# Self-attention and involution on one TensorE-bound core: v computed with pixels on partitions, and four smaller changes of order

## Chip, cores and metric

The kernel runs on one core of a Trainium2 chip. The metric is device time in microseconds, the median of three runs.

## What is computed

Two layers on x of shape (4, 512, 64, 64), all in f32. The first is single-head self-attention over the 4096 pixels of each image with 128 inner channels, and a residual. The second is an involution block: a 1x1 convolution to 128 channels with relu, then for every pixel a 7x7 filter for each of 8 groups of 16 channels, itself computed from that pixel, then a 1x1 convolution back to 512 channels and a residual.

```python
q = einsum('oc,bcn->bon', wq, xf) + bq            # k, v alike: 128 x 4096
attn = softmax(einsum('bci,bcj->bij', q, k), axis=-1)
out = einsum('bcj,bij->bci', v, attn)
x = einsum('oc,bcn->bon', wo, out) + bo + x
o = relu(affine(conv1x1(x, W1), s1, b1))          # 512 -> 128
w = conv1x1(relu(affine(conv1x1(o, Wr), sr, br)), Ws) + bs   # 49 taps x 8 groups
o = einsum('bgkhw,bgckhw->bgchw', w, patches(o))  # 7x7, zero padded
x = affine(conv1x1(o, W3), s3, b3) + x
```

## The kernel before, in words

All work is in `fast_path`; a second, general path runs only if a row sum of the softmax leaves a safe range, which it does not here. The images are done one after the other (L635). An image is eight chunks of 512 pixels.

**Keys and values** (`keys_values`, L420). For each chunk, four matmuls of 512 columns over the four channel tiles give pk (keys, channels on partitions), and four more give pv, values with channels on partitions. Attention needs v with pixels on partitions, so ScalarE copies pv to vs (L458), and one chunk later `turn` (L424) transposes it in four pieces on TensorE into pvt, which ScalarE copies to vT (L429). The bias of v is folded into the output bias: pb and bo, L639 to L643, once at image 0.

**Attention** (`attention`, L576). For each block of 512 queries (the last of the last image is cut into two of 256) there are 32 steps of 128 keys: a score matmul pss, exp on ScalarE into one of five pt buffers (L594), the product po with v, and on VectorE the sum of pt into pacc (L625); the last sum of a block is sums (L628).

**Finishing a block** (`finish_block`, L473) is a generator. Row sums become blocks, pl, rls and spread; four matmuls pwo (L511) are followed by four residual additions into x on VectorE (L513); then p1 (in the profile p, L520) and relu make the 128 channels, pp transposes them, and they are written to a padded image pix in DRAM (L548); pr and red prepare the filters. Each `yield` hands control back: one step is taken per call of `chores`.

**Involution** (`involution`, L280). A unit is four image rows with all 128 channels; an image has 16. The rows with their seven shifted copies are read from pix into a ring of 12 rows in SBUF (`pump`, L219: as many rows in one transfer as have been written and as the ring has room for). The filters of a unit are pw. For each tap column, VectorE multiplies 1, 2, 3 or 4 filter rows of ring data with pw into one of four prod buffers (L330), and GpSimd adds the product to acc (L354). After attention, in the tail, every second product is added on TensorE instead (accp, L350). `turn_unit` (L371) transposes acc (pa), and for every two units `close_chunk` (L401) does four matmuls py, four residual additions on VectorE (L408) and the store.

**The order of work** is written out by the Python program with a running estimate of TensorE's time, `pe`, in microseconds. `chores` (L248) is called after every step of attention and after every second matmul of keys and values; it takes one step of finishing, one of closing, and lets `pace` (L212) emit taps. `due` grows with TensorE's time; `involution` holds a tap back while VectorE's or GpSimd's estimated backlog is over 3.5 or 7.5 us, or its rows have not landed (L308). In the last image, `late` makes finishing wait for times instead of counting steps. Each engine takes its instructions in the order in which they were emitted, apart from small moves by the scheduler that builds the program. PSUM tiles pa, pwo, py, p, pp, pr, pl, spread and pq share two buffers, tag "mm"; acc and po have one each.

**The start.** vec goes on ScalarE's DMA queue; wk, then x of the first chunk in four pieces, wv, the next x and the other weights go on SyncE's (L171 to L179). GpSimd fills ones, the identity and zero.

Of the kernel before, what the change touches and what calls it, by code (L numbers as in the profile page):

```python
# [8 lines left out]
F32 = mybir.dt.float32  # L9
# [4 lines left out]
B, C, H, W = 4, 512, 64, 64  # L14
# [54 lines left out]
DVE_TAPS, POOL_TAPS = (0.16, 0.27), (0.19, 0.55)  # L69
ROW_US, X_US, PIX_US, LAND_US = 2.2, 3.8, 1.5, 3.0  # L70
HOP_US = 0.8
TB = 32

SAFE = (1e-30, 1e20)

# [2 lines left out]
def fast_path(  # L78
# [78 lines left out]
    def pe_us(us):  # L157
        nonlocal pe
        pe += us
# [8 lines left out]
        nc.sync.dma_start(xs[b, c], x_r[b, :, :, c * CH : (c + 1) * CH])  # L168


    nc.scalar.dma_start(vec, vecs)  # L171
    nc.sync.dma_start(wt[:, :O_WV], wts[:, :O_WV])
    c0, c1 = KEYS[:2]
    xs = {(0, c0): xpool.tile([P, CT, CH], F32, tag="x", name=f"x_0_{c0}")}
    for t in range(CT):
# [1 line left out]
    nc.sync.dma_start(wt[:, O_WV:O_WQ], wts[:, O_WV:O_WQ])  # L177
    load_x(0, c1)
    nc.sync.dma_start(wt[:, O_WQ:], wts[:, O_WQ:O_WR])  # L179
    nc.gpsimd.memset(ones, 1.0)  # L180
    make_identity(nc, ident)
    nc.gpsimd.memset(zero, 0.0)
    for i in range(P // TB):
# [8 lines left out]
    def w_slice(off, t):  # L192
        return wt[:, off + t * P : off + (t + 1) * P]
# [17 lines left out]

    def pace():  # L212
        nonlocal due, seen
        due, seen = min(due + TAPS_A_US * (pe - seen), 20), pe
        for _ in range(2):
            if due < 2 or not step(taps, 1):
                break

    def pump():  # L219

        nonlocal load
        while load // STEP in written:
            b, row = divmod(load, STEP)
            rows, us = written[b]

            end = H + SR - UR if rows == H else rows + PAD - 1
            n = min(b * STEP + end, low + RING) - load
            n = min(n, RING - load % RING)
            if n <= 0:
                break  # L230
            for h in range(2):
                src = pix[b % 2][row + h : row + h + n, :W, :]
                windows = bass.AP(
                    tensor=src.tensor, offset=src.offset, ap=[[P, W], [WP * P, n], [1, K * P]]
                )
                nc.sync.dma_start(
                    ring[h * W : (h + 1) * W, load % RING : load % RING + n]
                    .rearrange("p r x c -> p r (x c)"),
                    windows,
                )  # L240
            free["dma"] = max(free["dma"], us)
            us = takes("dma", ROW_US * n) + LAND_US
            landing.update((load + i, us) for i in range(n))
            load += n
            if row + n == H + SR - UR:
                load = (b + 1) * STEP
# [33 lines left out]
    def involution():  # L280
        nonlocal low, due
        while True:
# [15 lines left out]
            for o, (x, dy, n) in enumerate(ops):  # L298
                if o and dy >= DYS[1][0] > ops[o - 1][1]:
                    low = base + UR  # L300
                    pump()
                    if tail and units:
                        early[units[0]] = weights(*units[0])
                rows = [(base + dy + t * 2) % RING for t in range(NT)]
                while base + dy + n + NT > load:
                    yield "wait"
                landed = max(landing[base + dy + i] for i in range(n + NT))
                while not tail and (  # L308
                    pe < max(begin, landed)
                    or free["dve"] > pe + 3.5  # L310
                    or free["pool"] > pe + 7.5
                ):
                    yield "wait"
                free["pool"] = max(free["pool"], takes("dve", DVE_TAPS[0] + DVE_TAPS[1] * n))
                takes("pool", POOL_TAPS[0] + POOL_TAPS[1] * n)
                due -= n
                d0 = dy - DYS[dy >= DYS[1][0]][0]
                first = x == 0 and dy < DYS[1][0]
                prod, p0 = acc, d0
                if not first:  # L320
                    prod, p0 = prods.tile(
                        [P, NT, 4, P], F32, tag="prod", name=f"prod_{b}_{u}_{o}"
                    ), 0
                col = (x * K + dy) * G
                lines = ring[:, rows[0] : rows[0] + n, x, :]
                image = bass.AP(
                    tensor=lines.tensor, offset=lines.offset,
                    ap=[lines.ap[0], [(rows[1] - rows[0]) * K * P, NT], [K * P, n], [1, P]],
                )
                nc.vector.tensor_tensor(  # L330
                    prod[:, :, p0 : p0 + n, :].rearrange("p t d (g c) -> p t d g c", g=G),
                    image.rearrange("p t d (g c) -> p t d g c", g=G),
                    pw[:, :, col : col + n * G].unsqueeze(3)
                    .broadcast_to([P, NT, n * G, GC])
                    .rearrange("p t (d g) c -> p t d g c", d=n),
                    ALU.mult,
                )
                if first:
                    pass
                elif tail and o % 2 and (accp is not None or n > 1):  # L340

                    begin_sum = accp is None
                    if begin_sum:
                        accp = ps1.tile(
                            [P, NT, 2, P], F32, tag=("po", "acc")[u % 2], name=f"accp_{b}_{u}"
                        )
                    for d in range(0, n, 2):
                        k = min(2, n - d)
                        mm(
                            accp[:, :, :k, :], ident, prod[:, :, d : d + k, :],  # L350
                            begin_sum and d == 0, o + 2 >= len(ops) and d + 2 >= n,
                        )
                else:
                    nc.gpsimd.tensor_tensor(  # L354
                        acc[:, :, d0 : d0 + n, :], acc[:, :, d0 : d0 + n, :], prod[:, :, :n, :],
                        ALU.add,
                    )
                yield
# [61 lines left out]
    def keys_values(b):  # L420
        kt = kvpool.tile([P, N], F32, tag="k", name=f"k_{b}")
        vT = kvpool.tile([P, N // P, P], F32, tag="v", name=f"v_{b}")

        def turn(c, vs):  # L424
            pvt = ps1.tile([P, 4, P], F32, tag="acc", name=f"pvt_{b}_{c}")
            for j in range(4):
                nc.tensor.transpose(pvt[:, j, :], vs[:, j * P : (j + 1) * P], ident)
            pe_us(0.5)
            nc.scalar.copy(vT[:, 4 * c : 4 * c + 4, :], pvt)  # L429

        last = None
        for i, c in enumerate(KEYS):
            for k in KEYS[i + 1 : i + 3]:
                if (b, k) not in xs:
                    load_x(b, k)
            if b < 2 and i == 4:
                for rows in (slice(0, PAD), slice(PAD + H, None)):
                    nc.sync.dma_start(pix[b][rows].rearrange("r w c -> w r c"), zero)
                for cols in (slice(0, PAD), slice(PAD + W, None)):
                    nc.sync.dma_start(pix[b][PAD : PAD + H, cols, :], zero[:H])  # L440
            xt = xs[b, c] if c < KEEP else xs.pop((b, c))
            pk = ps_s.tile([P, CH], F32, tag="s", name=f"pk_{b}_{c}")
            for t in range(CT):
                mm(pk, w_slice(O_WK, t), xt[:, t, :], t == 0, t == CT - 1)
                if t % 2:
                    chores()
            nc.scalar.activation(
                kt[:, c * CH : (c + 1) * CH], pk, AF.Identity, bias=v1(V_BK)
            )
            if last is not None:  # L450
                turn(*last)
            pv = ps1.tile([P, CH], F32, tag="po", name=f"pv_{b}_{c}")
            for t in range(CT):
                mm(pv, w_slice(O_WV, t), xt[:, t, :], t == 0, t == CT - 1)
                if t % 2:
                    chores()
            vs = work2.tile([P, CH], F32, tag="q", name=f"vs_{b}_{c}")
            nc.scalar.copy(vs, pv)  # L458
            last = c, vs
        turn(*last)  # L460
        return kt, vT

    def queries(b, c, off, n):
# [9 lines left out]
    def finish_block(b, c, off, n, po, sums):  # L473
# [35 lines left out]
        for t in range(CT):  # L509
            pw = ps.tile([P, CH], F32, tag="mm", name=f"pwo_{name}_{t}")[:, :n]  # L510
            mm(pw, w_slice(O_WO, t), on)  # L511
            takes("dve", DVE_OP * n / CH)
            nc.vector.scalar_tensor_tensor(  # L513
                xt[:, t, :], pw, bo[:, t : t + 1], xt[:, t, :], ALU.add, ALU.add
            )
            for _ in range(t % 2 if late else 1 + (t != 1)):
                yield
        p1 = ps.tile([P, CH], F32, tag="mm", name=f"p1_{name}")[:, :n]
        for t in range(CT):
            mm(p1, w_slice(O_W1, t), xt[:, t, :], t == 0, t == CT - 1)  # L520
# [531 lines left out]
```

## Time and profile before

| | |
|---|---|
| time, median of 3 | 2656.51 us (2656.22 to 2658.48) |
| span of the profiled run | 2655.1 us |
| granted TensorE clock, mean | 0.997 |
| TensorE busy | 2625.3 us, 99% |
| VectorE, GpSimd, ScalarE busy | 1847.3, 1815.1, 886.5 us |
| DMA moved | 231.60 MB, mean 87 GB/s |
| ring reads, transfers of 1344 / 896 / 448 / 224 KB, median to landing | 15.3 / 13.4 / 8.7 / 3.3 us |

The profile is of one execution. Its parts are the busy time of each engine, the span in 40 slices, the DMA queues, the chain of work that ended last, the groups of instructions, and the DMA issues; the trace behind it answers for waits and for the timeline of any stretch. In those lines an instruction is named by line, tiles (out<-in) and shape; PE is TensorE's matmuls and PEld its weight loads, DVE VectorE, ACT ScalarE, POOL GpSimd. A line of the waits reads: engine, tile and line that waited <- what it waited for: microseconds in total, times, longest. A bracket at the end of a timeline line gives the engine's idle time before that group and what ended it. Each f32 matmul appears as two MATMUL and two LDWEIGHTS records.

### The profile page before, as it was taken

Reading aid. Unit: us, or ns where it says so; the run is one execution under the profiler, and the core shown is the slowest. Engines: PE = TensorE matmul, PEld = TensorE weight load, DVE = VectorE, ACT = ScalarE, POOL = GpSimd, SP = SyncE. Lnnn points to the kernel's source line nnn. Section 1 sums busy time; section 2 is a strip of 40 time slices with the busy share of each in tenths; the row PEclk is TensorE's granted clock in tenths of the full one; section 3 lists DMA queues with packets and bytes.
Section 4 is the critical chain, followed back from the end, with each engine's and each line's share of the span. In section 5 each row is a group of like instructions: output and inputs, shape, how many; then the busy total and the mean of one; then the engine's idle time right before and its main releaser. Section 6 shows DMA issues by size and latency. Waiting matters only on the chain.

```text
span 2655.1 us, 22780 instructions
## 1 busy us (share of the span) xinstructions
PE 2625.3 (99%) x6834; PEld 1197.4 (45%) x6834; DVE 1847.3 (70%) x2601; ACT 886.5 (33%) x1486; POOL 1815.1 (68%) x1195
## 2 busy tenths in 40 slices
PE   9999999999999999999999999999999999999998
PEld 4444444444444444444444444444444444444574
DVE  0347788786565777778566677778747577777877
ACT  2333333332333333333233333333323333333330
POOL 0007788787851878878774487878778277888865
PEclk9999999999999999999999999999999999999999
DMA  6032323235604233332450433333452423322243
GB/s 231 0 74 60 88 70 77 61 70 139 159 32 105 60 91 91 91 90 72 125 135 19 86 67 84 91 91 91 102 151 78 105 60 91 79 58 58 55 100 98
DMA packets 104260, 231.60 MB, mean 87 GB/s; under 512 B 5240, under 2 KB 23872, under 8 KB 104000
## 3 DMA queue, kind: packets, MB, share of 16 engines
q1 hardware_dynamic: 103984, 229.96, 35.2%
q8 instruction: 56, 0.92, 0.2%
q14 instruction: 76, 0.62, 0.1%
q10 hardware_dynamic: 144, 0.10, 0.0%
HBM read 187.28 MB, written 42.77 MB: 87 GB/s over the span
## 4 chain that ended last, share of the span: by engine, by line
PE 90%; POOL 4%; DMA 3%; DVE 2%; issue 1%; SPq 0%; ACT 0%; POOLq 0%; DVEq 0%; ACTq 0%
PE pss L200 33%; PE po L200 33%; PE p L200 4%; PE pwo L200 4%; PE py L200 4%; POOL acc L354 4%; PE pq L200 4%; DMA ring<-pix 2%; PE pw L200 2%; PE pv L200 2%; PE pk L200 2%; DVE prod L330 1%; DMA out_dram<-x 1%; PE accp L200 1%; PE pr L200 1%
## 5 line engine op out<-in xcount | busy, mean ns | idle before, releaser
L354 POOL TENSOR_TENSOR acc<-acc,prod 128x768 f32<-128x768 f32 (+3 forms) x1060 | 1693.2, 1615 | 814.6 <-DVE prod L330 629.5
L200 PE MATMUL pss<-q,k 128*128 128x512 f32 (+1 forms) x2112 | 1056.0, 585 | 0.0
L200 PE MATMUL po<-pt,v 128*128 128x512 f32 (+1 forms) x2112 | 1046.9, 580 | 0.0
L594 ACT ACTIVATE pt<-pss 128x512 f32<-128x512 f32 x1024 | 611.2, 597 | 1222.6 <-PE pss L200 1201.5
L625 DVE TENSOR_TENSOR pacc<-pacc,pt 128x512 f32<-128x512 f32 x958 | 666.1, 695 | 468.9 <-ACT pt L594 462.3
L330 DVE TENSOR_TENSOR prod<-ring,pw 128x512 f32<-128x512 f32 (+3 forms) x1092 | 898.8, 848 | 110.0 <-POOL acc L354 63.1
L200 PEld LDWEIGHTS po<-pt,v 128*128 128x128 f32 x2112 | 398.7, 190 | 478.5 <-issue 459.3
L200 PEld LDWEIGHTS pss<-q,k 128*128 128x128 f32 x2112 | 388.9, 190 | 454.6 <-issue 445.9
L408 DVE SCALAR_TENSOR_TENSOR x<-py,vec,x 128x512 f32<-128x512 f32 (+1 forms) x132 | 96.5, 732 | 64.5 <-PE py L200 62.3
L200 PE MATMUL py<-accT,wt 128*128 128x512 f32 (+1 forms) x264 | 131.7, 583 | 0.7 <-ACT accT L393 0.5
L200 PE MATMUL pwo<-on,wt 128*128 128x512 f32 (+1 forms) x264 | 129.9, 585 | 0.1
L200 PE MATMUL p<-x,wt 128*128 128x512 f32 (+1 forms) x264 | 122.5, 593 | 7.3 <-DVE x L513 7.3
L365 POOL TENSOR_TENSOR acc<-acc 128x512 f32<-128x512 f32 x120 | 119.8, 999 | 9.4
L200 PE MATMUL pk<-x,wt 128*128 128x512 f32 x256 | 119.5, 604 | 4.9 <-DMA x<-x_dram 4.9
L529 ACT ACTIVATE x<-x,vec 128x512 f32<-128x512 f32 (+1 forms) x132 | 92.9, 706 | 93.0 <-PE p L200 88.1
L200 PE MATMUL pv<-x,wt 128*128 128x512 f32 x256 | 116.8, 593 | 0.0
L200 PE MATMUL pq<-x,wt 128*128 128x512 f32 (+1 forms) x264 | 115.8, 579 | 0.0
L513 DVE SCALAR_TENSOR_TENSOR x<-pwo,bo,x 128x512 f32<-128x512 f32 (+1 forms) x132 | 95.9, 731 | 22.4 <-PE pwo L200 20.5
L330 DVE TENSOR_TENSOR acc<-ring,pw 128x1024 f32<-128x1024 f32 (+1 forms) x84 | 79.1, 961 | 46.5 <-PE pw L200 46.4
L200 PEld LDWEIGHTS p<-x,wt 128*128 128x128 f32 x264 | 50.6, 193 | 68.9 <-issue 56.8
L200 PEld LDWEIGHTS pwo<-on,wt 128*128 128x128 f32 x264 | 51.2, 194 | 61.5 <-issue 55.4
L200 PEld LDWEIGHTS pk<-x,wt 128*128 128x128 f32 x256 | 48.7, 194 | 64.6 <-issue 58.4
(58 smaller groups left out, 798.1 us busy)
## 6 DMA issues: line engine op xcount, KB each, us to landing
x<-x_dram SPq DMA_DIRECT2D x55, 1024.0 KB, 5.7
ring<-pix SPq DMA_DIRECT2D x32, 1344.0 KB, 15.3
ring<-pix SPq DMA_DIRECT2D x72, 448.0 KB, 8.7
out_dram<-x SPq DMA_DIRECT2D x31, 1024.0 KB, 4.2
ring<-pix SPq DMA_DIRECT2D x32, 896.0 KB, 13.4
ring<-pix SPq DMA_DIRECT2D x8, 2240.0 KB, 24.8
pix<-o1t SPq DMA_DIRECT2D x62, 128.0 KB, 2.5
ring<-pix SPq DMA_DIRECT2D x8, 224.0 KB, 3.3
```

The lines of the kernel that those rows point to most:

```text
L200: return nc.tensor.matmul(o, lhsT=lhsT, rhs=rhs, start=start, stop=stop)
L330: nc.vector.tensor_tensor(prod[:, :, p0 : p0 + n, :].rearrange("p t d (g c) -> p t d g c", g=G), image.rearrange("p t d (g c) -> p t d g c ...
L354: nc.gpsimd.tensor_tensor(acc[:, :, d0 : d0 + n, :], acc[:, :, d0 : d0 + n, :], prod[:, :, :n, :], ALU.add,)
L365: nc.gpsimd.tensor_tensor(acc[:, :, :n, :], acc[:, :, :n, :], acc[:, :, n : 2 * n, :], ALU.add)
L408: nc.vector.scalar_tensor_tensor(xt[:, t, :], py, v1(V_S3 + t), xt[:, t, :], ALU.mult, ALU.add)
L513: nc.vector.scalar_tensor_tensor(xt[:, t, :], pw, bo[:, t : t + 1], xt[:, t, :], ALU.add, ALU.add)
L529: nc.scalar.activation(xt[:, t, :], xt[:, t, :], AF.Identity, bias=v1(V_B3 + t))
L594: nc.scalar.activation(pt, pss, AF.Exp)
L625: nc.vector.tensor_tensor(paccs[k], paccs[k], pt, ALU.add)
```

## The change

1. **v at once.** The pixels of x become the stationary operand (128 of a chunk at a time) and wv the moving one, so that the product has pixels on partitions from the start: 16 matmuls of 128 columns instead of four of 512, in a PSUM tile that alternates between the tags po and acc; pvt and the copy to vs go.
2. **Pace.** `pace` may emit 2 taps plus one per microsecond of TensorE's time since the last call, instead of 2; in the last image VectorE's backlog may be 4.5 us instead of 3.5.
3. **Later use of the residual.** In all images but the last, two more steps go by between the last residual addition of a block and p1, which reads x.
4. **Lead-in.** Eight matmuls on ones, whose result nobody reads, are put ahead of everything on TensorE; ones is filled by VectorE; wk comes in two pieces on ScalarE's queue, ahead of vec, so that x is first on SyncE's.
5. **Ring rows by three.** In the last image one transfer into the ring holds at most three rows.

```diff
+STEP_US = 1.0
+PIECE = 3
+WARM = 8
...
+    for cols in (slice(0, P), slice(P, O_WV)):
+        nc.scalar.dma_start(wt[:, cols], wts[:, cols])
     nc.scalar.dma_start(vec, vecs)
-    nc.sync.dma_start(wt[:, :O_WV], wts[:, :O_WV])
...
-    nc.gpsimd.memset(ones, 1.0)
+    nc.vector.memset(ones, 1.0)
+
+    warm = ps.tile([P, P], F32, tag="mm", name="warm")
+    for _ in range(WARM):
+        nc.tensor.matmul(warm, lhsT=ones, rhs=ones, start=True, stop=True)
...
     def pace():
         nonlocal due, seen
+        steps = 2 + int((pe - seen) / STEP_US)
         due, seen = min(due + TAPS_A_US * (pe - seen), 20), pe
-        for _ in range(2):
+        for _ in range(steps):
...
-            n = min(n, RING - load % RING)
+            n = min(n, RING - load % RING, PIECE if b == B - 1 else RING)
...
-                    or free["dve"] > pe + 3.5
+                    or free["dve"] > pe + (4.5 if b == B - 1 else 3.5)
...
-        def turn(c, vs):
-            pvt = ps1.tile([P, 4, P], F32, tag="acc", name=f"pvt_{b}_{c}")
-            for j in range(4):
-                nc.tensor.transpose(pvt[:, j, :], vs[:, j * P : (j + 1) * P], ident)
-            pe_us(0.5)
-            nc.scalar.copy(vT[:, 4 * c : 4 * c + 4, :], pvt)
...
-            if last is not None:
-                turn(*last)
-            pv = ps1.tile([P, CH], F32, tag="po", name=f"pv_{b}_{c}")
-            for t in range(CT):
-                mm(pv, w_slice(O_WV, t), xt[:, t, :], t == 0, t == CT - 1)
-                if t % 2:
+            pv = ps1.tile([P, 4, P], F32, tag=("po", "acc")[i % 2], name=f"pv_{b}_{c}")
+            for j in range(4):
+                for t in range(CT):
+                    mm(
+                        pv[:, j, :], xt[:, t, j * P : (j + 1) * P], w_slice(O_WV, t),
+                        t == 0, t == CT - 1,
+                    )
+                if j % 2:
                     chores()
-            vs = work2.tile([P, CH], F32, tag="q", name=f"vs_{b}_{c}")
-            nc.scalar.copy(vs, pv)
-            last = c, vs
-        turn(*last)
+            nc.scalar.copy(vT[:, 4 * c : 4 * c + 4, :], pv)
...
+        for _ in range(0 if late else 2):
+            yield
         p1 = ps.tile([P, CH], F32, tag="mm", name=f"p1_{name}")[:, :n]
```

More of the change, by code (lines that the diff above doesn't have):

```diff
@@ L422, in keys_values @@
         vT = kvpool.tile([P, N // P, P], F32, tag="v", name=f"v_{b}")
-        def turn(c, vs):
-            pvt = ps1.tile([P, 4, P], F32, tag="acc", name=f"pvt_{b}_{c}")
-            for j in range(4):
-                nc.tensor.transpose(pvt[:, j, :], vs[:, j * P : (j + 1) * P], ident)
-            pe_us(0.5)
-            nc.scalar.copy(vT[:, 4 * c : 4 * c + 4, :], pvt)
-        last = None
         for i, c in enumerate(KEYS):
```

## The prediction

> **What bounds the kernel now.** I read the page's first part, then the waits of the TensorE, then the timeline of the start, of the first image change, and of the end.
>
> ```profile
> PE 2625.3 (99%) x6834; PEld 1197.4 (45%) x6834; DVE 1847.3 (70%) x2601; ACT 886.5 (33%) x1486; POOL 1815.1 (68%) x1195
> PE p L200 <- DVE x L513: 7.3, 3, 2.5
> PE pk L200 <- DMA x<-x_dram: 4.9, 1, 4.9
> PE accp L200 <- DVE prod L330: 4.0, 4, 2.3
> PE pw L200 <- DVE prod L330: 2.1, 2, 1.4
> ```
>
> TensorE is the bound until attention ends (last sums at 2564.11): up to there it waits only for its first operands (4.9 us), three times for p at image changes (7.3) and for a few pw. After it, the last four units' taps on VectorE run to 2639.27, and a chain of copies, py and stores ends at 2655.1. So three things count: TensorE's work, its waits, and how many taps are left for the tail.
>
> ```profile
> 2564.11 0.69 DVE L628 TENSOR_TENSOR sums<-pacc,pt 128x512 f32<-128x512 f32 x1 [1.03 <-ACT pt L594]
> 2639.27 1.06 DVE L271 TENSOR_SCALAR ok<-rls 128x512 f32<-128x512 f32 x1
> ```
>
> ```profile
> 4.88 6.20 PE L200 MATMUL pk<-x,wt 128*128 128x512 f32 x8 [4.88 <-DMA x<-x_dram]
> 17.79 0.60 PE L427 MATMUL pvt<-ident,vs 128*128 128x128 f32 x4
> 18.22 3.60 PE L200 MATMUL pv<-x,wt 128*128 128x512 f32 x8
> 66.77 0.97 PEld L200 LDWEIGHTS pb<-vec,wt 128*128 128x128 f32 x8
> 2642.49 1.05 PE L200 MATMUL pa<-ident,acc 128*128 128x128 f32 x8
> 2643.38 0.61 PE L200 MATMUL pa<-ident,accs 128*128 128x128 f32 x4
> 2643.82 1.06 PE L200 MATMUL pa<-ident,acc 128*128 128x128 f32 x8
> 2644.72 0.61 PE L200 MATMUL pa<-ident,accs 128*128 128x128 f32 x4
> ```
>
> Columns: start, time, engine, instruction. Each f32 matmul shows as two passes. Eight passes of 512 columns take 3.43 us start to start (0.429 each), the first pk 6.2; four transposes 0.43; 20 passes of 128 columns with a new weight each (2642.49 to 2644.72) 2.23, or 0.1115 each. Eight loads for pb, whose products have one column, take some 0.89: 0.111 each, so a weight load sets that rate.
>
> The first image change, time from E = 626.03, the end of the old image's last po:
>
> ```profile
> 624.10 13.15 POOL L354 TENSOR_TENSOR acc<-acc,prod 128x768 f32<-128x768 f32 x7 [3.94 <-DVE prod L330]
> 637.33 2.08 POOL L365 TENSOR_TENSOR acc<-acc 128x512 f32<-128x512 f32 x2
> 639.96 27.75 POOL L354 TENSOR_TENSOR acc<-acc,prod 128x1024 f32<-128x1024 f32 x13 [0.55 <-DVE prod L330]
> 658.30 0.95 DVE L330 TENSOR_TENSOR prod<-ring,pw 128x768 f32<-128x768 f32 x1 [0.93 <-POOL acc L354]
> 659.18 0.74 DVE L513 SCALAR_TENSOR_TENSOR x<-pwo,bo,x 128x512 f32<-128x512 f32 x1
> 659.97 1.98 PE L200 MATMUL p<-x,wt 128*128 128x512 f32 x4 [2.42 <-DVE x L513]
> ```
>
> GpSimd adds without a pause; each product needs one of four prod buffers; the fourth residual (x at L513) stands on VectorE behind such a product; p needs it, also because p's PSUM tile is the one pwo held.
>
> **The skill.** "TensorE: Matmul & The Clock Gate", LDWEIGHTS, prices a weight load by its columns, 128/1.2 = 107 ns, and lets it run under the matmul before it; the trace has 0.111 for f32. The same page, Part 1, says that the array starts at half rate and is released after about 3.4 us of activity: the first pk's passes are 0.85 apart, later ones 0.43, and the switch falls near 9.7, 4.8 us after the start. Its table of queues has VectorE as strict FIFO, which the residual behind the products shows.
>
> **The change, part by part.**
>
> *v at once.* Removed per chunk: 8 passes of 512 (3.43), 4 transposes (0.44), one ScalarE copy. Added: 32 passes of 128: 3.57 at 0.1115. Saved 0.30 a chunk, 32 chunks: 9.6 us. Bounds: 0.107 a pass, the transposes' pace, gives 14; 0.118, at which the 16 pa passes from 2606.63 to 2608.52 went, gives 3. ScalarE loses a copy of 0.58 a chunk and is 33% busy: nothing on the path. At image 0 also the wait for vs before pb (0.73) goes. So image 0: 8 x 0.30 + 0.7 = 3.1.
>
> *Lead-in.* Eight f32 matmuls on ones are 16 passes; at half rate 0.22 each, from about 1.0 to 4.5, while wk and x land. If release follows activity as before, it comes near 6 rather than 9.7: pk starts near 4.5, has under two cold passes, ends near 8.7 instead of 11.0. Saved 2.3 (1 to 3.3). wk as two pieces on the ScalarE queue starts x 0.46 sooner; within that. By the bytes moved, the second x is in by 10.7, and is needed at 12.3.
>
> *Image change (two more yields).* In the built order p moves behind the next pv, but the py of an older chunk (the second of four) now takes the PSUM tile that pwo's fourth held, and its wait in the built program is that fourth residual. When is it there? VectorE now has all seven 768-element products of unit 11 behind sums and blocks, whose end is near E-0.4. GpSimd then starts at E+0.5: 13.15 + 2.08 + six 1024 adds (2.43 each, 14.6) + one 768 (1.88), then a product 0.95 and the residual 0.7: E+33.9. When is it wanted? TensorE has 3.43+0.14+3.57+3.43+0.86 (pk, pl, pv, pk, pw), 3.57+0.86 (pv, pwo), 3.43+1.72 (pk, two pwo), 0.22+3.57 (pa, pv), 1.72 (pwo, py), 3.43 (pk): E+30.0. It waits 3.9, against 2.4 before. (Same sums for before: residual 659.9, p wanted 657.4: as seen.) Behind that py stand pv, p and all of the phase. The residual chain belongs to GpSimd, so what v saves before the wait is waited again. Whole phase, E to the first pss: 80.3 before; after, 2.4 less for v, 0.9 for a pw that moves later (not saved), 0.7 for its wait, 2.4 for p's wait, plus 3.9 and 0.8 for q's copy that nothing covers now: net -0.8 each, three: -2.4. The later pix write (E+51 instead of E+46) delays ring rows to about E+74; pacc's first copy then comes near E+84, and the five pt buffers need it by E+87: no wait.
>
> *Pace.* A step of attention is four passes, 1.72 us, so three taps instead of two may go per call; the guard of 3.5 us is unchanged for images 0 to 2, the taps done by the end of each block are the same within 20 rows, and VectorE (70%) and GpSimd (68%) work beside TensorE: nothing. For image 3 the guard is 4.5: VectorE may lag 1 us more. Behind the longer queue stand pacc, which frees pt for the next exp, and the residuals of pwo, which free the PSUM tiles of later pwo; TensorE waits for both. Before, no such wait shows in image 3; there are nine blocks, so taken +1, bounds 0 to 4.
>
> *Tail.* I counted the taps that stand behind the last blocks in VectorE's built order, in output rows of one filter row: 196 before (four whole units of 49), 165 after. The 31 are seven products of 1024 (1.13 apart) and one of 768 (0.87); one py residual (0.67) goes ahead too: 9.4 us less VectorE work behind the last sums. But the seven come in a burst ahead of it: from one pacc to sums stand five pacc (0.6 each), seven products (7.9) and the py residual (0.7), 11.6, where TensorE takes five steps of 1.72, 8.6; and the first waits some 0.5 for its pw. So the last sums run 3.5 late, and the tail ends 5.9 earlier (3 to 9: with the lag doubled, or with none). VectorE's pauses in the tail, some 6 us in all, I leave as they are. Rows by three cuts up loads: two-row loads take 8.7 (median), four-row ones 13.4, and the first row that unit 14's second half needs from a freed slot is wanted some 15 us after the slot is free; hidden, with little to spare, so no gain and no loss. The last 16 us, from the end of the taps to the end of the stores, are the same instructions.
>
> Sum: -3.1 - 2.3 - 2.4 + 1.0 - 5.9 = -12.7, from 2656.5: 2644.
>
> **Rivals.**
> (A) The wait at image changes is gone: taps' products start earlier, or the py is not held. Then 3 x 3.9 more: about 2632. For: p had only 2.4 to lose, and the two yields are meant for it. Against: the PSUM tile and the sums above. Chance 0.2.
> (B) What the burst and the guard win in taps is lost again in image 3 (pacc behind products, residuals late), and the tail gains nothing: +3 and 0 instead of +1 and -5.9: 2652. For: the waits of VectorE's products for GpSimd are 63 us already, and whatever stands behind such a product waits too. Against: five pt buffers bear five steps, 8.6 us, of lag. Chance 0.16.
> (C) Slower: weight loads do not hide under 128-column passes. At 0.19 + 0.107 a pass, pv costs 9.5 a chunk instead of 3.57, 32 chunks +190: about 2834. A milder form, 0.13 a pass because x as weights and a PSUM tile shared with attention disturb the flow, costs 1024 passes x 0.0185 = +19: 2663. Speaks for it that one load alone lasts 190 ns; against it the pa groups, whose passes with a new weight each start 0.1115 apart. Together 0.08.
> Mine 0.56.
>
> **How the numbers follow.** 2644 is the likeliest. The range 2630 to 2654 takes in A and B and the ends of v (-4.6 more), tail and lead-in; C is left out. Faster than 2651.2: mine, A and 0.05 of B, 0.81; between 2651.2 and 2661.8: the rest of B, 0.11; slower: C, 0.08.
>
> **What would show it.** v: 32 passes of pv in 3.5 to 3.6 us. Lead-in: first pv near 8.7. Image change: no wait of p, but three waits of py for x at L513's counterpart, about 4 us each; if py waits under 1 us, A is right. Image 3: TensorE waits over 1 us in all before the last sums speak for B. Tail: from the end of attention to the end 82 us, before 88. Wrong most likely where GpSimd's chain starts elsewhere than E+0.5, since every us of it moves the time by three.

## The result, and the profile after

The changed kernel takes 2644.95 us (median of 5, 2644.45 to 2645.81) against 2658.48 (5 runs, 2656.22 to 2661.26) for the kernel before on the same chip: ratio 0.9948, 95% interval 0.9937 to 0.996. The profiled spans are 2643.6 and 2655.1 us. By stages of the two timelines, in us:

| stage | before | after | difference | forecast |
|---|---|---|---|---|
| start to the first pss of image 0 | 72.21 | 67.09 | -5.12 | -5.4 |
| three image changes, first pk to first pss | 80.42, 81.60, 82.88 | 80.57, 81.89, 80.83 | -1.61 | -5.0 |
| attention of images 0 to 2, pss to next pk | 1679.86 | 1680.21 | +0.35 | +1.7 |
| image 3, first pss to last sums | 567.14 | 570.68 | +3.54 | +5.4 |
| last sums to the end of the taps (ok) | 75.16 | 67.18 | -7.98 | -9.4 |
| from there to the end | 15.83 | 15.15 | -0.68 | 0 |
| sum | | | -11.5 | -12.7 |

The prediction's -0.8 an image change counts a pw of 0.86 us back in, because it only moves behind the first scores. By stages its terms are thus -1.7 an image change and +0.86 in each attention that follows. The traces have the pw there: each image change has 8 passes of pw instead of 12, the attention of images 1 and 2 has 56 instead of 52, and image 3 from its first pss on 72 instead of 68.

The lines of after that answer to those shown of before. First the page's busy times, then TensorE's waits (total, times, longest):

```profile
PE 2614.5 (99%) x7478; PEld 1254.9 (47%) x7478; DVE 1851.5 (70%) x2602; ACT 870.0 (33%) x1454; POOL 1821.4 (69%) x1197
```

```profile
PE py L208 <- DVE x L513: 12.7, 3, 4.5
...
PE pss L208 <- ACT q L469: 2.3, 3, 0.8
```

The three waits of p (7.3) are gone; three waits of py for the same residual stand in their place, and they are longer. TensorE's timeline, at the start and at the first image change:

```profile
1.64 3.20 PE L188 MATMUL warm<-ones 128*128 128x128 f32 x14
4.63 4.74 PE L208 MATMUL pk<-x,wt 128*128 128x512 f32 x8
9.21 3.73 PE L208 MATMUL pv<-wt,x 128*128 128x128 f32 x32
...
646.97 3.60 PE L208 MATMUL pk<-x,wt 128*128 128x512 f32 x8
654.52 1.30 PE L208 MATMUL py<-accT,wt 128*128 128x512 f32 x2 [3.95 <-DVE x L513]
655.61 5.24 PE L208 MATMUL pv<-wt,x 128*128 128x128 f32 x32
660.69 1.88 PE L208 MATMUL p<-x,wt 128*128 128x512 f32 x4
```

The first pv starts at 9.21 and the next pk at 12.78: 3.57 for 32 passes. After the wait of py the same 32 passes take from 655.61 to 660.69, 5.08. VectorE and GpSimd at that change, and VectorE at the end:

```profile
652.85 0.95 DVE L339 TENSOR_TENSOR prod<-ring,pw 128x768 f32<-128x768 f32 x1 [0.93 <-POOL acc L363]
653.72 0.75 DVE L513 SCALAR_TENSOR_TENSOR x<-pwo,bo,x 128x512 f32<-128x512 f32 x1
...
2561.27 0.68 DVE L630 TENSOR_TENSOR sums<-pacc,pt 128x512 f32<-128x512 f32 x1
2628.45 1.06 DVE L280 TENSOR_SCALAR ok<-rls 128x512 f32<-128x512 f32 x1
```

```profile
621.11 13.17 POOL L363 TENSOR_TENSOR acc<-acc,prod 128x768 f32<-128x768 f32 x7 [4.96 <-DVE prod L339]
634.36 2.08 POOL L374 TENSOR_TENSOR acc<-acc 128x512 f32<-128x512 f32 x2
636.40 27.75 POOL L363 TENSOR_TENSOR acc<-acc,prod 128x1024 f32<-128x1024 f32 x13
```

GpSimd adds without a pause, the fourth residual stands behind a product that waits for GpSimd, and it ends 34.15 us after the last po. The slow passes after the wait show in the table of stretches, whose third number from the end is the granted clock:

```profile
core 0: us, PE busy (x) PEld busy (x) DVE busy (x) ACT busy (x) POOL busy (x), PEclk, DMA share, GB/s
654.40:657.90 3.50, 3.38 (x13) 2.77 (x14) 2.85 (x5) 0.00 (x0) 3.34 (x3) 0.64 0.00 0
1299.40:1302.90 3.50, 3.39 (x10) 2.36 (x11) 2.86 (x5) 0.00 (x0) 3.34 (x3) 0.50 0.00 0
```

In the kernel before, four passes of p take 1.82 us behind its first wait, but 3.51 and 3.09 behind the second and third, whose lines the prediction does not show. The second:

```profile
1303.52 3.68 PE L200 MATMUL p<-x,wt 128*128 128x512 f32 x4 [2.45 <-DVE x L513]
1307.03 1.03 PE L200 MATMUL py<-accT,wt 128*128 128x512 f32 x2
```

Two questions come out of this. Is the wait of py made by the PSUM tile that it takes, and does it bring the half-rate passes with it? And is each part worth what the sum gave it?

### The profile page after: what moved, and what is told of

Its sections match the earlier page's. It is cut to its first block, busy times and chain, and to the rows that moved or that the text cites. A ratio compares the mean times of both kernels' runs of the same rounds, so it can differ in the third digit from the quotient of the medians.

```text
span 2643.6 us, 24069 instructions
## 1 busy us (share of the span) xinstructions
PE 2614.5 (99%) x7478; PEld 1254.9 (47%) x7478; DVE 1851.5 (70%) x2602; ACT 870.0 (33%) x1454; POOL 1821.4 (69%) x1197
## 4 chain that ended last, share of the span: by engine, by line
PE 91%; POOL 4%; DMA 2%; DVE 2%; issue 1%; ACT 0%; SPq 0%; POOLq 0%; DVEq 0%; ACTq 0%
PE pss L208 32%; PE po L208 32%; POOL acc L363 4%; PE pq L208 4%; PE p L208 4%; PE py L208 4%; PE pwo L208 4%; PE pv L208 3%; PE pk L208 3%; DMA ring<-pix 2%; PE pw L208 2%; DVE prod L339 1%; PE pr L208 1%; PE pp L543 1%; PE accp L208 0%
## 5 line engine op out<-in xcount | busy, mean ns | idle before, releaser
L208 PE MATMUL py<-accT,wt 128*128 128x512 f32 (+1 forms) x264 | 133.0, 587 | 13.8 <-DVE x L513 12.7
L208 PEld LDWEIGHTS pv<-wt,x 128*128 128x128 f32 x1024 | 123.3, 198 | 14.8 <-issue 14.8
L208 PE MATMUL pv<-wt,x 128*128 128x128 f32 x1024 | 126.0, 282 | 0.0
L531 ACT ACTIVATE x<-x,vec 128x512 f32<-128x512 f32 (+1 forms) x132 | 92.9, 706 | 81.5 <-PE p L208 76.3
L208 PEld LDWEIGHTS py<-accT,wt 128*128 128x128 f32 x264 | 49.5, 191 | 72.9 <-issue 43.3
L208 PEld LDWEIGHTS pq<-x,wt 128*128 128x128 f32 x264 | 49.7, 190 | 58.8 <-issue 52.7
```

The costliest lines, as they stand in the source:

```text
L208: return nc.tensor.matmul(o, lhsT=lhsT, rhs=rhs, start=start, stop=stop)
L531: nc.scalar.activation(xt[:, t, :], xt[:, t, :], AF.Identity, bias=v1(V_B3 + t))
```

## The experiments

**1. What does the wait of py cost?** Closing (pa, py) is held at image changes from the fourth pwo until p is issued, so no second py takes that pwo's PSUM tile; and a variant with one more step before p.

```diff
+    def chores(kv=False):
         step(finishing, 1)
-        step(closing, 1)
+        if not (kv and held):
+            step(closing, 1)
...
+        if not late:
+            held.append(name)
         for _ in range(0 if late else 2):      # 3 in the variant
             yield
+        held.clear()
         p1 = ps.tile(...)
```

> The changed kernel, but at image changes closing (pa and py) stops from the fourth pwo until p is issued, so that the second py does not take the PSUM tile of the fourth pwo. Theory (the tile makes the wait of 3.95 to 4.55 us, and that wait costs another 1.5 to 2 us of half-rate passes): p is wanted about 3.6 us later than that py was, waits 0.3 to 1 us for the residual, no half-rate passes follow, and three times 4.7 to 5.5 us are saved: 2629 to 2631. Rival (what is saved is waited again before the next image's scores, for q, ring rows or pacc): 2640 or more.

> As the kernel with closing held from the fourth pwo until p, with three steps instead of two before p, so that half a pk goes ahead of p as well. Theory: p does not wait at all, 3 x 5 to 6 us saved against the changed kernel: 2627 to 2630, some 1 us less than with two steps. Rival: py heaps up later in the image change or the next image's rows come too late for pacc, and it is slower than with two steps.

Measured: 2628.05 us with two steps (ratio to before 0.9887, 0.9872 to 0.9902), 2624.1 with three (0.987, 0.9855 to 0.9885), both below what was expected. TensorE's timeline with two steps, the three places where p waits, and VectorE's residual there:

```profile
653.81 1.98 PE L209 MATMUL p<-x,wt 128*128 128x512 f32 x4 [0.31 <-DVE x L515]
...
1293.70 1.98 PE L209 MATMUL p<-x,wt 128*128 128x512 f32 x4 [1.00 <-DVE x L515]
...
1932.89 1.98 PE L209 MATMUL p<-x,wt 128*128 128x512 f32 x4 [0.64 <-DVE x L515]
```

```profile
652.14 0.95 DVE L341 TENSOR_TENSOR prod<-ring,pw 128x768 f32<-128x768 f32 x1 [0.94 <-POOL acc L365]
653.01 0.74 DVE L515 SCALAR_TENSOR_TENSOR x<-pwo,bo,x 128x512 f32<-128x512 f32 x1
```

The residual ends 34.1 us after the last po, as in the changed kernel; only its first user comes later. The wait falls from 12.7 to 2.0 us in all, the passes after it run at full rate (p's four take 1.82), and the three image changes last 75.3, 76.3 and 75.6 us instead of 80.6, 81.9 and 80.8. That is 16.1 us less, 10.7 of waiting and 5.4 of half-rate passes. py reads accT and wt and not x, so its tile alone ties it to the residual: the PSUM tile made the wait, and nothing took it back. With three steps p does not wait at all, but not for the reason I gave:

```profile
647.53 0.74 DVE L515 SCALAR_TENSOR_TENSOR x<-pwo,bo,x 128x512 f32<-128x512 f32 x1
...
654.45 1.88 PE L209 MATMUL p<-x,wt 128*128 128x512 f32 x4
```

There the built order also has three products fewer ahead of the residual, which ends at 648.27, over 6 us before p needs it.

**2. Is it the idle that slows the passes?** TensorE is kept active in the wait (the pv tile is made earlier for it, which the cut leaves out):

```diff
+                if b and i == 3 and t == 3:
+                    for _ in range(15):
+                        nc.tensor.matmul(pv[:, 0, :], lhsT=ones, rhs=ones, start=True, stop=True)
                 if t % 2:
                     chores()
```

> The changed kernel with 15 matmuls of 128 columns on ones (30 passes, 3.35 us; nobody reads them) into the next pv tile ahead of the py that waits at each image change. The residual that py waits for comes no sooner. Theory (an idle of some 4 us puts TensorE back to half rate for about 3.4 us): with TensorE active in the wait, the 32 passes of pv after it take 3.6 us instead of 5.1, the rest of the wait is 0.5 to 1.2 us, and the time is 4 to 5.7 us less: 2639 to 2641. Rival (the passes after the wait are slow for another reason, such as their operands or what VectorE does then): those 32 passes take 5 us as before, and the time does not move.

Measured: 2641.36 us, ratio 0.9935 (0.9921 to 0.9948), against 0.9948 for the changed kernel: some 3.5 us less, though the intervals overlap. The timeline at the first change, and the granted clock behind the py at all three:

```profile
654.58 1.12 PE L209 MATMUL py<-accT,wt 128*128 128x512 f32 x2 [0.97 <-DVE x L517]
655.54 3.73 PE L209 MATMUL pv<-wt,x 128*128 128x128 f32 x32
659.11 1.88 PE L209 MATMUL p<-x,wt 128*128 128x512 f32 x4
```

```profile
654.50:659.10 4.60, 4.52 (x34) 4.04 (x35) 3.16 (x5) 0.00 (x0) 4.37 (x4) 1.00 0.00 0
1298.70:1303.30 4.60, 4.53 (x34) 4.05 (x35) 3.15 (x5) 0.00 (x0) 4.37 (x4) 1.00 0.00 0
1943.40:1948.00 4.60, 4.52 (x34) 4.04 (x35) 3.16 (x5) 0.00 (x0) 4.37 (x4) 1.00 0.02 4
```

py starts at the same time as before, so the residual came no sooner; the 32 passes after it take 3.57 at a clock of 1.00. The rival cause falls. The gain is under the forecast: full rate saves 5.4 us at the three changes, but pa now waits 2.3 us at two of them.

**3. Each part taken out of the changed kernel.** In turn: the old v; no added steps; no matmuls on ones and the old DMA order; two taps per call and a guard of 3.5; ring rows as many as fit.

```diff
-        for _ in range(0 if late else 2):                 # no added steps
-            yield
...
-        steps = 2 + int((pe - seen) / STEP_US)            # old pace
+        steps = 2
...
-                    or free["dve"] > pe + (4.5 if b == B - 1 else 3.5)
+                    or free["dve"] > pe + 3.5
...
-            n = min(n, RING - load % RING, PIECE if b == B - 1 else RING)    # rows as fit
+            n = min(n, RING - load % RING)
```

> The changed kernel with the old making of v (four 512-column products, four transposes, two copies a chunk); all else as changed. My theory (the TensorE time per chunk is what counts, 3.43 + 0.44 against 3.57): 9.6 us more over 32 chunks, plus 0.7 for the wait before pb, less some 0.9 at each of three image changes, because what v saves ahead of the waiting py is waited again: 7 to 8 us slower than the changed kernel, 2652 to 2653; the wait of the second py for the fourth residual about 3.0 us each instead of 3.95 to 4.55. Rival (the new v buys nothing, because weights from x and PSUM tiles shared with attention cost elsewhere what it saves): within 2 us of the changed kernel.

> The changed kernel without the two added steps between the last residual and p, so that p is again what waits for the fourth residual. Theory 1 (the wait belongs to the residual, which GpSimd's chain of adds sets, and only moves from p to py): p waits 2.5 to 3.1 us at each image change, no py waits, and the time is 1 to 4 us less than the changed kernel, 2641 to 2644, because one more py lies ahead of the wait. Theory 2 (the two steps do what they are for): 3 x 2 us or more slower, 2651.

> The changed kernel without the eight matmuls on ones, with the old DMA order and GpSimd filling ones. Theory: pk starts near 4.9 and passes at half rate, first pv at 11.0 instead of 9.2: 1.9 us slower, all of it in the first 12 us, 2647. Rival: a later wait (x of the second chunk, or the weights) takes it back, and the time does not move.

> The changed kernel with two taps per call and a guard of 3.5 us in the last image too. Theory (31 row-taps more are left for the tail, last sums 3.5 us earlier): 4 to 6 us slower, 2649 to 2651, with the end of the taps about 9 us later after the last sums. Rival B (a burst ahead of the last sums costs there what the tail wins): within 1.5 us of the changed kernel.

> The changed kernel with ring rows of the last image again in transfers of as many rows as fit. Theory (transfers are hidden): within 1 us of the changed kernel. Rival (rows come too late for the taps in the tail, and three at a time start them sooner): 2 us or more slower, with waits of products for the ring in the last 120 us.

| without | time | ratio to before (95%) | image changes |
|---|---|---|---|
| v at once | 2656.03 | 0.9991 (0.9985 to 0.9998) | 82.42, 84.69, 84.26 |
| the two steps | 2646.95 | 0.9957 (0.9943 to 0.997) | 83.22, 82.73, 82.83 |
| the lead-in | 2647.64 | 0.9955 (0.9942 to 0.9969) | 81.14, 81.75, 81.27 |
| pace and guard | 2656.54 | 0.9993 (0.9986 to 1.0) | 85.68, 85.51, 85.65 |
| rows by three | 2647.12 | 0.9958 (0.9945 to 0.9972) | 81.92, 82.49, 81.31 |

The ratios less 0.9948 come to some 11, 2, 2, 12 and 3 us; the five add to 30, over twice the 13.8 that 0.9948 stands for. The intervals of the three small ones overlap that of the changed kernel; the two large ones stand clear of it and alone make 23. So the parts are not separate terms. With the old v, py waits 3.25, 4.25 and 3.94 us, not the 3.0 that I expected, and the slow passes after it cost 6.6 us in all, so that it is 11 us and not 7 to 8. Without the lead-in the first pv starts at 10.13 and the first pss at 68.02, against 66.4 to 67.1 in eight runs with lead-in and the new v: 0.9 to 1.6 us. In the changed kernel pk starts 0.24 us sooner than without the lead-in, and its eight passes take 4.58 instead of 5.26, so most of the gain is in the rate of the passes. Without rows by three image 3 and its tail are 0.4 us longer; another 2.4 us lie at the image changes, where TensorE's order is the same in both: behind waits of the same length (12.5 and 12.7) half-rate passes lose 7.8 us instead of 5.7. A difference of 2 to 3 us between two kernels can thus come from the half-rate passes alone. The surprise is the pace. TensorE's waits and one line of its timeline without it:

```profile
PE pk L208 <- DMA x<-x_dram: 22.1, 3, 7.5
```

```profile
692.75 5.28 PE L208 MATMUL pk<-x,wt 128*128 128x512 f32 x8 [7.53 <-DMA x<-x_dram]
```

No py waits for a residual any more; pk waits for x, and runs at half rate after it (5.1 us for 3.43). Neither of my theories had this wait. Without the two steps it is there too (11.8 us in all), and p waits 3.6 us in all, less than half of what I expected. The tail is as short as in the changed kernel (66.6 us), so the pace is not what shortened it.

**4. Where does the wait for x come from?** SyncE's queue at the first change without the pace (time, length, line, transfer):

```profile
666.31 1.26 SPq L550 DMA_DIRECT2D pix<-o1t  x2
668.97 0.39 SPq L426 DMA_DIRECT2D out_dram<-x  x1
669.46 3.46 SPq L245 DMA_DIRECT2D ring<-pix  x4
673.01 0.63 SPq L171 DMA_DIRECT2D x<-x_dram  x1
```

and in the changed kernel:

```profile
670.25 0.38 SPq L426 DMA_DIRECT2D out_dram<-x  x1
673.36 1.26 SPq L550 DMA_DIRECT2D pix<-o1t  x2
674.72 0.56 SPq L171 DMA_DIRECT2D x<-x_dram  x1
675.85 4.38 SPq L245 DMA_DIRECT2D ring<-pix  x6
```

In the changed kernel the image's last x (1 MB) goes out ahead of all ring rows and lands 8.1 us after its issue. Without the pace it goes out behind four ring transfers (2.7 MB) and lands 19.6 us after it. To test whether the place is the cause, the old pace is kept and only this load is emitted one chunk sooner, which leaves TensorE's order as it was but for one pw at each image change, which moves behind the first scores:

```diff
-            for k in KEYS[i + 1 : i + 3]:
+            for k in KEYS[i + 1 : i + (4 if i == 4 else 3)]:
```

> The changed kernel with the old pace and guard, as in the run without them, and one thing more: the load of an image's last chunk of x is emitted one chunk earlier, which moves it ahead of the four transfers of ring rows on SyncE's queue and leaves TensorE's order as it was. Theory Q (the wait of pk for x, 7.3 to 7.5 us three times, comes from that place in the queue): the wait is gone, and with it the half-rate passes after it: 22 to 28 us less than without the pace, 2628 to 2635. Rival (the x is late because its buffer comes free late, and the place does not matter): pk waits as before, within 3 us of 2656.5. Second rival (ring rows come later by as much, and pacc or the taps wait instead): 2645 or more.

Measured: 2631.58 us, ratio 0.9898 (0.9882 to 0.9913), 25 us less than with the load in its old place. The queue, the pk that had waited, and VectorE around the fourth residual:

```profile
665.96 1.26 SPq L550 DMA_DIRECT2D pix<-o1t  x2
668.62 0.39 SPq L426 DMA_DIRECT2D out_dram<-x  x1
670.67 0.37 SPq L171 DMA_DIRECT2D x<-x_dram  x1
671.10 7.43 SPq L245 DMA_DIRECT2D ring<-pix  x6
...
684.71 3.60 PE L208 MATMUL pk<-x,wt 128*128 128x512 f32 x8
```

```profile
649.09 0.95 DVE L339 TENSOR_TENSOR prod<-ring,pw 128x768 f32<-128x768 f32 x1 [1.47 <-POOL acc L363]
649.97 0.74 DVE L513 SCALAR_TENSOR_TENSOR x<-pwo,bo,x 128x512 f32<-128x512 f32 x1
```

The load goes out only 2.3 us earlier, and pk no longer waits for it. The last two lines show what the new pace does at an image change: with the old one the residual starts at 649.97, behind three 768-element products after the last 1024-element one; with the new one at 653.72, behind five. Two products at GpSimd's 1.88 us are 3.76; counted from the last po the residual is 3.4 us later. With the old pace the second py is also wanted 1.6 us later (31.9 us after the last po, not 30.2). Most of the wait of py in the changed kernel is thus made by its pace.

**5. v alone, rows by three alone**, each put on the kernel before.

> The kernel before with the new making of v and nothing else. In its built order the load of the last chunk of x of each image change stands on SyncE's queue behind the store of an old chunk and behind transfers of ring rows, where in the kernel before and in the changed kernel it stands ahead of all ring rows. Theory Q (the place in the queue decides, as in the runs without the pace and without the two steps, where pk waited 4 to 7.5 us for x): 2.4 to 3.1 us saved at image 0, but pk waits 4 to 8 us for x at each of three image changes, which then last 84 to 86 us instead of 80.4 to 82.9: 2660 to 2668, slower than before. Simple theory (only TensorE's time per chunk counts): 9.6 + 0.7 saved, 2646 to 2648.

> The kernel before with ring rows of the last image by three and nothing else. In its built order 172 row-taps instead of 196 are left behind the last sums, as they are with the pace alone or the guard alone. Theory R (rows by three, more taps per call and the guard each bring the taps forward, and any one is enough): the tail from the last sums to the end of the taps lasts about 67 us instead of 75, the last sums come 3 us later, 4 to 6 us faster than before, 2651 to 2653. My prediction's view (rows by three do nothing, the pace does it): within 1.5 us of before.

v alone: 2657.5 us, ratio 0.9999 (0.999 to 1.0007). The first pss comes 4.0 us sooner (68.21), and then:

```profile
PE pk L200 <- DMA x<-x_dram: 17.9, 4, 5.0
...
PE p L200 <- DVE x L504: 3.3, 3, 1.1
```

13.0 of the 17.9 us are at the image changes (5.05, 3.99, 3.92), which last 85.0, 82.9 and 82.5 us. The queue theory named the cause, and gave it 3 to 10 us too much in all: the waits were at its lower end, p's wait shrank, and from the last sums to the end of the taps it took 74.0 us instead of 75.2.

Rows by three alone: 2652.75 us, ratio 0.9984 (0.9975 to 0.9992). VectorE's last sums and the end of the taps:

```profile
2567.77 0.69 DVE L628 TENSOR_TENSOR sums<-pacc,pt 128x512 f32<-128x512 f32 x1
2635.81 1.06 DVE L271 TENSOR_SCALAR ok<-rls 128x512 f32<-128x512 f32 x1
```

The tail lasts 68.0 us instead of 75.2 and image 3 570.1 instead of 567.1: nearly the whole effect that I had given to the pace, 4 us net. So rows by three are enough by themselves, and the run without them showed that the pace and guard are too (66.6 us). In built orders that were not run, the guard alone or the taps per call alone also leave 172 row-taps instead of 196; whether either shortens the tail as much was not measured.

**6. A better version.** On the kernel with closing held and three steps, the first queries of an image go between the last pk and the last pv:

```diff
+            if c == 0:
+                early_q[b] = queries(b, 0, 0, CH)
             pv = ps1.tile(...)
...
-        qs[0] = queries(b, *blocks[0])
+        qs[0] = early_q.pop(b)
```

> The kernel with closing held until p and three steps before p, with the first queries of an image (pq and the copy q) put between the last pk and the last pv, so that the copy to q lies beside pv. Theory: the three waits of the first pss for q (0.78 us each) and the one at image 0 are gone: 2 to 3.5 us less than without it, 2621 to 2622. Rival (the copies of k, q and v on ScalarE come in a row, and the first po waits for v instead): no change.

Measured: 2621.1 us, ratio 0.9858 (0.9843 to 0.9873), 3.0 us less than without it; no pss waits for q. The intervals of the two overlap, but each of the three image changes is shorter by 0.94 us in the traces (73.58 instead of 74.52). By the medians it is 24 us faster than the changed kernel, which itself gained 13.5.

## Why the prediction was right, and where not

The time was forecast at 2644 and is 2644.95. The mechanisms at the start and of the wait came out as worked; the account of which edit does what did not. The closeness of the total is in part luck: by stages, the image changes came out 3.4 us and the tail 1.4 us worse than forecast, and attention of images 0 to 2, image 3 and the end 1.4, 1.8 and 0.7 us better.

- **v's passes: right.** 3.57 us for 32. From the first pv to the first pss of image 0 it took 61.29 before, 57.88 after: 3.4 against the 3.1 forecast. Rival C is refuted.
- **Lead-in: right, a little less.** First pv 1.7 us sooner than before (10.92 to 9.21), 0.9 against the run without the lead-in; over all runs it starts at 8.5 to 9.2 in ten with the lead-in, at 10.1 to 11.3 in four without. Forecast 2.3, bounds 1 to 3.3.
- **The wait moved to py: right.** Forecast: residual at E+33.9, wait 3.9. Measured E+34.15, and waits of 3.95, 4.55 and 4.22, 12.7 in all for 11.7. The wait for q was 0.78 for 0.8.
- **Net -0.8 an image change: the failed term.** Counted like the forecast, with the moved pw, the three changes came to +1.0 and not to -2.4 (-1.61 in the table, and 3 x 0.86). One of the missing 3.4 us is the longer waits of py, and 2.0 are passes at half rate: I priced a wait at its length. Counted from starts of instructions against full rate, the passes behind the three waits of py lose another 1.74, 2.20 and 1.73 us; those behind p in the kernel before lost 0.10, 1.79 and 1.80, which I missed too, since I read only its first change and took it for all three. "TensorE: Matmul & The Clock Gate", Part 1, in the Trainium skill, has the other half of what I used for the lead-in: after an idle window of about 3.4 us the array is back at half rate, and the window runs free. Experiment 2 agrees for waits near 4 us. Waits of 2.45 us are shorter than that window, and yet slow passes followed two of the three in the kernel before; why is open. The harm was small because attention and image 3 came out shorter than forecast, for which, the missing wait of the guard apart, the runs show no reason.
- **"Pace: nothing" in images 0 to 2: wrong.** It puts two more products ahead of the fourth residual, which is most of the wait of py; and without it the last x falls behind ring rows. I read VectorE's new order rightly but booked the wait under the two steps. I also looked for lost time in TensorE's and VectorE's orders and not in SyncE's.
- **v's 9.6 us as a term of its own: wrong.** In the changed kernel it is there because the last x still goes out first; alone it is worth nothing. As the runs show, v with the old pace, or v without the two steps, has the x behind ring rows; v with both has it ahead.
- **Tail: right in size.** Net -4.4 (3.54 later, 7.98 shorter), or -5.3 without the pw that came over to image 3, against -4.9. The cause was shared: "rows by three: 0" holds beside the pace, not alone. The +1 for the guard's extra waits was not seen: between its first scores and the last sums of image 3 TensorE has one wait of 0.46 us, and in the kernel before one of 0.32. Rival B is refuted.
- **Rival A** asked what no wait would give, and said 2632. It gave 2628 and 2624, as the half-rate passes go with the wait.

On the transfers, "DMA: Bandwidth & Descriptors", Queues, rings and completion order, in the Trainium skill, says that each DMA engine takes the descriptors of a ring in order; 19.6 us behind ring rows and 8.1 ahead of them agree.

## What to carry to other kernels

Taking a part out of a change measures that part in its company: when the five do not add up, look for an order they set together, and read the order of the load queue as closely as that of the engines. Price a wait of TensorE of some 3 us or more at its length plus about 2 us of half-rate passes (1.5 to 3.1 in these runs), and first ask whether the waiting instruction needs the result or only its buffer. A queue place costs one line to test: move the one transfer and leave the rest.

## What the runs showed of the hardware that was not expected

At the image changes of seven runs TensorE waited 21 times for 3.25 us or more (py for its tile, or pk for x, up to 7.5). Each wait was followed by 1.5 to 3.1 us lost to half-rate passes, and the loss varied where order and wait were the same. Before the last sums, waits of 0.3 to 1.4 us were followed by none. Of six waits of p of 2.42 to 2.45 us, three in the kernel before and three with rows by three alone, four were. A 1 MB load issued 2.3 us earlier, ahead of four transfers instead of behind them, was there at least 8 us earlier (needed at 684.71 without a wait, where it had been waited for until 692.75).
